# An attention layer in fixed order: its two GRUs as a pipeline, W_gat folded into weights, and 1/degree by logarithm and Newton

## The chip, the cores and the metric

One core of a Trainium2 chip runs the whole program. The metric is device time in microseconds of one execution of the kernel; lower is better. Engines are named as in the profile: PE is TensorE's matrix multiplication and PEld its loading of weights, DVE is VectorE, ACT is ScalarE, POOL is GpSimd and SP is SyncE, which here only issues DMAs. A name with q, such as ACTq, is an engine's own sequencer or DMA queue. L12 is line 12 of the kernel before.

## The reference

Four graph layers in a row work on x (3327 nodes by 64 numbers) with one adjacency matrix of 0 and 1. Each layer is x = x + layer(relu(layernorm(x))). Layers 0 and 3 are hyperbolic attentions; layer 1 is a decaying sum over neighbours; layer 2 is a graph attention with two GRUs. With the weights at hand, the matrix has no negative entries, and this is what layer 2 comes to:

```python
def gru_cell(x, h, w_ih, w_hh, b_ih, b_hh):
    gi = x @ w_ih.T + b_ih
    gh = h @ w_hh.T + b_hh
    ir, iz, inn = jnp.split(gi, 3, axis=1)
    hr, hz, hn = jnp.split(gh, 3, axis=1)
    r = jax.nn.sigmoid(ir + hr)
    z = jax.nn.sigmoid(iz + hz)
    n = jnp.tanh(inn + r * hn)
    return (1.0 - z) * n + z * h
...
node_support = jnp.concatenate([(A_node > 0).astype(h.dtype) @ h, (A_node < 0).astype(h.dtype) @ h], axis=1)
edge_output = gru_cell(node_support, h, w_ih_e, w_hh_e, b_ih_e, b_hh_e)
edge_support = gat(h, A_node, A_edge, W_gat, a_gat)
node_output = gru_cell(edge_support, h, w_ih_n, w_hh_n, b_ih_n, b_hh_n)
return d_edge[:, None] * edge_output + d_node[:, None] * node_output
```

The attention gives all neighbours of a node the same weight here, so that `gat` is (A @ h) @ W_gat divided by the node's degree.

## The kernel before, in words

Nodes are padded to 3328: 26 tiles of 128. The kernel runs four stages, and at the end a count of assumptions (ok) decides whether a slower general version must run as well.

Layer 0 (`hyperbolic_series`, L304) reads the matrix in pieces and lasts until 284 us. Layer 1 (`plain_decay`, L1230) reads it again, in 52 quarters of 832 KB (`quarters`, L1201), keeps it on chip as 13 double tiles of one byte an element (`masks`), and sums with decaying weights. Layer 2 (`plain_gat`, L1374) and layer 3 take it from there.

In `plain_decay` a step is one quarter. DVE makes the mask (L1287), and, for the quarters that are not in the list `LATE` (13 of 52), counts the zeros (`zeros`, L1207), by which the kernel knows that there are only zeros and ones. PE counts neighbours (L1294), ACT takes powers of two (L1300), and PE sums (L1311). The order is written out by hand (`manual_schedule`): each of the named engines does its work in the order of the program, and masks are made two steps ahead. Four quarters are in flight (L1258), one is loaded when a buffer comes free. Ahead of the loop stand the norm (`norm_relu`, L111) and the splitting of its result H into two 16-bit parts (`split2`, L164), and behind it ACT copies the degrees (L1316), a product turns the sums back (L1195) and DVE adds them to X (L1320). POOL adds the bias to X (L1362) and clears the masks' diagonal (L178).

In `plain_gat` the order is not written out: a scheduler arranges the instructions of each engine by priority and readiness. There are these parts:

- the 13 late quarters are read again (L1394), four in flight, for their zero counts;
- the norm and the split of H;
- 416 products of the masks with the two parts of H into four banks (L1407), from the last row tile b = 25 down to 0;
- between them, at two places of that loop, the turning of H into columns (`to_pairs`, L1170), and the degrees: a count of those up to 100 (L1415), their sum (L1416), and for each of four pieces the subtraction of the diagonal (L1424), a clamp to 1 (L1425) and a reciprocal (L1426);
- ACT and DVE take the sums from the banks (L1434, L1435);
- the two GRUs (L1453 to L1475), g = 0 and g = 1, in four pieces of 416 columns each. Two groups of nodes lie in the upper and lower 64 partitions. The second GRU first multiplies its input with W_gat (L1447) and copies it on ACT (L1448);
- the turn back (L1193) and the addition to X (L1482, L1483).

The weights come through POOL's and ACT's DMA queues (`gru_weights`, L1209, and L1251 to L1254). `ball` (L274) makes the constants of a hyperbolic layer; for layer 3 it works from r on DVE (L295 to L301), after the degrees.

Of the kernel before, what the change touches and what calls it, by code (L numbers as in the profile page):

```python
# [46 lines left out]
def tile_gnn4(ctx: ExitStack, tc: tile.TileContext, x, adjT, att0, b0, w1, bias1, w_gat, a_gat,  # L47
# [63 lines left out]
    def norm_relu(pool, h, dst=None):  # L111

        s = pool.tile([P, T], F32, name="ln_s")
        v = pool.tile([P, T], F32, name="ln_v")
        sq = pool.tile([P, T, D], F32, name="ln_sq")
        for ts in HALVES:
            V.reduce_sum(s[:, ts], X[:, ts, :], axis=AX.X)
        V.tensor_scalar(s, s, 1.0 / D, None, op0=OP.mult)
        for ts in HALVES:
            V.tensor_sub(h[:, ts, :], X[:, ts, :], wide(s[:, ts]))  # L120
            A.activation(sq[:, ts, :], h[:, ts, :], AF.Square)
        for ts in HALVES:
            V.reduce_sum(v[:, ts], sq[:, ts, :], axis=AX.X)  # L123
# [3 lines left out]
        for o, ts in enumerate(HALVES):  # L127
            V.scalar_tensor_tensor(h[:, ts, :] if dst is None else dst[:, o], h[:, ts, :], 0.0, wide(sd[:, ts]),
                                   op0=OP.max, op1=OP.mult)

# [33 lines left out]
    def split2(pool, src, name):  # L164

        hi, lo = [pool.tile(list(src.shape), F16, name=f"{name}_{k}") for k in range(2)]
        n = src.shape[1] // 2
        for q in (slice(0, n), slice(n, src.shape[1])):
            A.activation(hi[:, q], src[:, q], AF.Copy, scale=SH)
            V.scalar_tensor_tensor(lo[:, q], src[:, q], SH, hi[:, q], op0=OP.mult, op1=OP.subtract)  # L170
        return hi, lo
# [102 lines left out]
    def ball(att, b_att, r, min_norm, min_norm2, after=None):  # L274

        k = "0" if r is None else "1"
# [13 lines left out]
        if r is None:  # L290
            for t, value in ((cc, 1.0), (sqc, 1.0), (isqc, 1.0), (um, 0.0), (maxn2, min_norm2)):
                V.memset(t, value)
        else:
            nc.scalar.dma_start(cc, bcast_rows(r))
            V.scalar_tensor_tensor(cc, after, -3e38, cc, op0=OP.min, op1=OP.max)  # L295
            V.tensor_mul(cc, cc, cc)
            V.reciprocal(cc, cc)
            V.tensor_copy(sqc, sqrt_(const, cc, "sq"))
            V.reciprocal(isqc, sqc)
            V.tensor_scalar(um, sqc, min_norm / MIN_NORM, None, op0=OP.mult)  # L300
            V.tensor_scalar(maxn2, cc, min_norm2, None, op0=OP.mult)  # L301
        return wlr, bcol, cc, sqc, isqc, um, maxn2

    def hyperbolic_series(r, params, ok, masks=None, done=None):  # L304
# [18 lines left out]
        with ExitStack() as st:  # L323
# [161 lines left out]
            with tc.tile_pool(name="hsw", bufs=2) as wk, tc.tile_pool(name="hsps", bufs=1, space=PSUM) as ps, \  # L485
# [60 lines left out]
                def sums(k):  # L546
# [15 lines left out]
                    if b == T - 1:  # L562
                        a = new("sum", c)
# [606 lines left out]
    def to_pairs(psum, dst, src, lower):  # L1170


        for t0 in range(0, T // 2, 4):
            n = min(4, T // 2 - t0)
            pt = psum.tile([P, 4 * P], F32, name="pt")
            for k in range(n):
                t = t0 + k
                PE.transpose(pt[:, k * P:(k + 1) * P], src[:, t, :, :].rearrange("p o d -> p (o d)"), ident)
            cs = slice(t0 * P, (t0 + n) * P)
            A.activation(dst[:, cs], pt[:, :n * P], AF.Copy)  # L1180
            for o in range(2):
                A.activation(lower[o][D:, cs], pt[o * D:(o + 1) * D, :n * P], AF.Copy)

    def from_pairs(psum, src, use, w=None, tiles=range(T // 2), pt=None):
# [24 lines left out]
    def gru_weights(pool):  # L1209

        wg = pool.tile([P, D], F32, name="wg")
        for o in (0, D):
            nc.gpsimd.dma_start(wg[o:o + D, :], w_gat)
        gru = []
        for wi, wh, bi, bh in ((wih_e, whh_e, bih_e, bhh_e), (wih_n, whh_n, bih_n, bhh_n)):
            g = len(gru)
            wt = pool.tile([P, 3, D], F32, name=f"gw{g}")
            bt = pool.tile([P, 6], F32, name=f"gb{g}")
            brz = pool.tile([P, 3], F32, name=f"gs{g}")
            nc.gpsimd.dma_start(wt[:D, :, :], wi[:D].rearrange("k (g m) -> k g m", g=3))  # L1220
            nc.gpsimd.dma_start(wt[D:, :, :], wh.rearrange("k (g m) -> k g m", g=3))
            for o in (0, D):
                q = slice(o, o + D)
                nc.gpsimd.dma_start(bt[q, :3], bi)
                nc.gpsimd.dma_start(bt[q, 3:], bh)
            G.tensor_tensor(brz, bt[:, :3], bt[:, 3:], op=OP.add)
            gru.append((wt, bt, brz))
        return wg, gru

    def plain_decay(masks, zo, deg):  # L1230
# [8 lines left out]
        K = 200.0  # L1239
        steps = [(c, b) for c in range(2) for b in range(T - 1, -1, -1)]  # L1240
        with ExitStack() as st:
# [7 lines left out]
            wt = pers.tile([P, P], F32, name="wt")  # L1249
            G.memset(wt, 0.0)  # L1250
            nc.scalar.dma_start(wt[:D, :D], w1)  # L1251
            nc.scalar.dma_start(wt[D:, D:], w1)
            bias = pers.tile([P, D], F32, name="bias")
            nc.scalar.dma_start(bias, bcast_rows(bias1, D))  # L1254
            adjs = {}

            def load(k):
                adjs[k] = wk.tile([P, 2, CW], F32, name="adj", bufs=4)  # L1258
                nc.sync.dma_start(adjs[k], quarters(k))

            for k in range(4):
# [9 lines left out]
            with tc.tile_pool(name="pdacc", bufs=1, space=PSUM) as pa, tc.manual_schedule(  # L1271
# [42 lines left out]
                def degrees(c, o):  # L1314
                    q = slice(o * D, (o + 1) * D)
                    A.activation(deg[q, c * CW:(c + 1) * CW].rearrange("p (h i) -> p h i", h=2),  # L1316
                                 cnt[o][q, :, :BK], AF.Copy)
# [11 lines left out]
                make_mask(1)  # L1329
                with tc.tile_pool(name="pdp", bufs=1) as tp:  # L1330
                    H = tp.tile([P, T, D], F32, name="H")
                    norm_relu(tp, H)
                    table_of(AF.Exp)
                    parts = split2(pers, H, "h2")
                for o in range(2):
                    cnt[o] = pa.tile([P, 2, 512], F32, name=f"cnt{o}")
                for k in range(K_ + 2):
# [19 lines left out]
                    if k + 2 < K_:  # L1357
                        make_mask(k + 2)
                        if k + 4 < K_:
                            load(k + 4)  # L1360
                    if k == 4:
                        G.tensor_tensor(X, X, bias[:, None, :].to_broadcast([P, T, D]), op=OP.add)  # L1362
# [11 lines left out]
    def plain_gat(masks, zo, deg, first, wg, gru):  # L1374
# [8 lines left out]
        with ExitStack() as st:  # L1383
            pers = st.enter_context(tc.tile_pool(name="pg", bufs=1))
            H = pers.tile([P, T // 2, 2, D], F32, name="H")
            hP = pers.tile([P, HP], F32, name="hP")

            xh = [pers.tile([P, HP], F32, name=f"xh{o}") for o in range(2)]
            oP = pers.tile([P, HP], F32, name="oP")
            wk = st.enter_context(tc.tile_pool(name="pgl", bufs=4))  # L1390
# [4 lines left out]
            with tc.tile_pool(name="pgp", bufs=1) as tp:  # L1395
                norm_relu(tp, tp.tile([P, T, D], F32, name="hn"), H.rearrange("p k o d -> p o k d"))
                parts = split2(pers, H, "h2")

            with tc.tile_pool(name="pgacc", bufs=1, space=PSUM) as pa, \
                    tc.tile_pool(name="pgps", bufs=2, space=PSUM) as ps:  # L1400
                acc = [pa.tile([P, BK], F32, name=f"acc{k}") for k in range(C)]
                for b in range(T - 1, -1, -1):
# [7 lines left out]
                    if b == T - 3:  # L1410
                        to_pairs(ps, hP, H, xh)
                    if b == T - 4:

                        few = wk.tile([P, HP], BF, name="few", bufs=1)
                        V.tensor_scalar(few, deg, 100.0, 0.0, op0=OP.is_le, op1=OP.add, accum_out=ok[:, 3:])  # L1415
                        V.reduce_sum(zo[:, 2 * T:], deg, axis=AX.X)  # L1416
                        V.tensor_mul(zo[:, 2 * T:], zo[:, 2 * T:], first)
                        for k in range(C):
                            cs = slice(k * BK, (k + 1) * BK)
# [149 lines left out]
```

## Time and profile before

| what | us |
|---|---|
| three runs, median | 829.16 |
| three runs, lowest and highest | 827.92, 830.69 |
| the profiled execution, its own time | 831.17 |
| its span, first to last instruction | 829.5 |
| DVE busy | 721.5 (87% of the span) |
| PE busy | 662.2 (80%) |
| ACT busy | 562.0 (68%) |
| POOL busy | 419.0 (51%) |

The profile is one execution. Busy time of PE is modelled. The shares are averages over stages with different limits, so that a change is to be looked for in its own stage. Layer 0 takes the first 284 us, the decay stage goes on to 429, the attention layer to 543, and layer 3 takes the rest. The chain that ended last, followed back from the last instruction, is 65% DVE, 14% PE, 7% DMA, 6% ACT and 5% issue.

### The profile page before, as it was taken

What the parts mean: (1) busy time and instruction counts of PE and PEld (TensorE: products, weight loads), DVE (VectorE), ACT (ScalarE), POOL (GpSimd) and SP (SyncE); (2) the same over time, 40 slices, a digit from 0 to 9 for tenths busy, and PEclk for the clock granted to TensorE, in tenths of its full rate; (3) what the DMA queues carried; (4) which work ended last, traced back from release to release, by engine and by line L of the source; (5) the groups of instructions that cost most, each with busy time, mean ns of one, the idle gap of its engine ahead of it and who ended that gap; (6) DMA issues with size and microseconds to landing.
All of it is one profiled execution on the core that took longest, in us unless ns stands there. A gap on an engine that the chain in (4) does not pass through costs nothing.

```text
span 829.5 us, 11810 instructions
## 1 busy us (share of the span) xinstructions
PE 662.2 (80%) x4228; PEld 251.2 (30%) x4228; DVE 721.5 (87%) x1013; ACT 562.0 (68%) x684; POOL 419.0 (51%) x283
## 2 busy tenths in 40 slices
PE   0889999999896059989970997618999999998940
PEld 0422233333331024435430662204222333333310
DVE  7689999999997999999989946796999999999966
ACT  3878888888884167777761306448888888888850
POOL 2499989989985310002300000004787777787720
PEclk9999999999999569999995899958999999999985
DMA  2577766767662639999943630002001001000001
GB/s 42 167 235 227 204 204 191 238 182 204 190 191 66 225 126 339 349 347 333 338 170 126 220 113 1 0 0 48 1 2 35 1 1 35 0 2 1 0 4 44
DMA packets 56887, 107.86 MB, mean 130 GB/s; under 512 B 8305, under 2 KB 32817, under 8 KB 56817
## 3 DMA queue, kind: packets, MB, share of 16 engines
q1 hardware_dynamic: 51712, 106.68, 40.2%
q10 hardware_dynamic: 4656, 0.08, 0.3%
q8 instruction: 35, 0.57, 0.3%
q0 software_dynamic: 448, 0.24, 0.1%
q14 instruction: 36, 0.29, 0.1%
HBM read 103.73 MB, written 0.88 MB: 126 GB/s over the span
## 4 chain that ended last, share of the span: by engine, by line
DVE 65%; PE 14%; DMA 7%; ACT 6%; issue 5%; POOL 2%; ACTq 1%; DVEq 0%; POOLq 0%
DVE sig L543 22%; DVE slot L542 20%; DMA adj<-in 7%; DVE same L1207 5%; PE acc L1407 5%; DVE mask L1287 3%; POOL sig L519 2%; PE slot L552 2%; ACT y L537 1%; DVE deg L1426 1%; PE cnt L1294 1%; DVE X L740 1%; DVE prod L739 1%; PE slot L560 1%; DVE ln_v L123 1%
## 5 line engine op out<-in xcount | busy, mean ns | idle before, releaser
L537 ACT ACTIVATE y<-slot,shift_c 128x768 f32<-128x768 f32 (+1 forms) x208 | 197.6, 950 | 69.7 <-ACT sig L517 48.1
L543 DVE TENSOR_TENSOR sig<-slot,sig 128x768 f32<-128x768 f32 (+1 forms) x208 | 213.2, 1025 | 24.7 <-POOL sig L519 2.7
L542 DVE SCALAR_TENSOR_TENSOR slot<-y,slot 128x768 f32<-128x768 f32 (+1 forms) x208 | 212.1, 1020 | 9.0 <-ACT y L537 8.9
L519 POOL TENSOR_TENSOR sig<-adj,sig 128x768 f32<-128x768 f32 (+1 forms) x104 | 201.8, 1962 | 24.8 <-ACT sig L517 14.7
L517 ACT ACTIVATE sig<-leftB,right 128x768 f32<-128x768 f32 (+1 forms) x208 | 204.1, 981 | 0.2
L519 POOL TENSOR_TENSOR sig<-mask,sig 128x768 f32<-128x768 fp8e4 (+1 forms) x104 | 174.6, 1680 | 57.2 <-ACT sig L517 53.1
L552 PE MATMUL slot<-sig,Xr 128*64 128x384 f32 (+1 forms) x832 | 187.2, 538 | 18.3 <-DVE sig L543 18.3
L530 PE MATMUL slot<-XC,XT 128*128 128x384 f16 (+1 forms) x416 | 142.1, 342 | 5.0 <-DVE sig L543 3.3
L531 PE MATMUL slot<-XF,XE 73*128 73x384 f16 (+1 forms) x416 | 141.4, 340 | 0.0
L1300 ACT ACTIVATE w<-cnt,ebias 128x832 bf16<-128x832 f32 x104 | 93.8, 950 | 32.4 <-PE cnt L1294 32.4
L1207 DVE TENSOR_SCALAR_CACHE_REDUCE same<-adj 128x1664 bf16<-128x1664 f32 x52 | 97.7, 1880 | 3.5 <-DMA adj<-in 3.5
L560 PE MATMUL slot<-sig,X 128*32 128x384 f32 (+1 forms) x832 | 95.0, 529 | 0.0
L468 POOL COPY Xp<-Xe 128x234 f16<-128x234 f16 x2 | 0.8, 415 | 160.1 <-DVE XT L414 146.4
L552 PEld LDWEIGHTS slot<-sig,Xr 128*64 128x64 f32 x832 | 42.9, 135 | 123.9 <-DVE sig L543 85.2
L1294 PE MATMUL cnt<-mask,after 128*128 128x416 fp8e4 x208 | 54.8, 347 | 25.3 <-DVE mask L1287 22.6
L178 POOL TENSOR_TENSOR mask<-mask,offdiag 128x128 fp8e4<-128x128 fp8e4 x26 | 16.8, 666 | 105.4 <-PE cnt L1294 104.2
L530 PEld LDWEIGHTS <-XT 128*128 128x128 f16 x416 | 40.6, 98 | 94.7 <-issue 68.8
L1294 PE MATMUL cnt<-mask,rest 128*128 128x416 fp8e4 x208 | 55.0, 347 | 12.5 <-ACT w L1300 12.5
L1287 DVE TENSOR_SCALAR mask<-adj 128x1664 fp8e4<-128x1664 f32 x52 | 53.3, 1031 | 6.7 <-DMA adj<-in 6.6
L531 PEld LDWEIGHTS <-XE 73*128 73x128 f16 x416 | 40.7, 98 | 33.3 <-issue 9.3
L1311 PE MATMUL acc<-w,h 128*64 128x416 bf16 x416 | 47.2, 349 | 0.0
L1407 PE MATMUL acc<-mask,h 128*64 128x416 fp8e4 x416 | 38.3, 346 | 0.1
(293 smaller groups left out, 547.7 us busy)
## 6 DMA issues: line engine op xcount, KB each, us to landing
adj<-in SPq DMA_DIRECT2D x65, 832.0 KB, 6.9
adj<-in SPq DMA_DIRECT2D x78, 384.0 KB, 3.9
adj<-in SPq DMA_DIRECT2D x27, 512.0 KB, 4.7
leftB<-left SPq DMA_DIRECT2D x6, 384.0 KB, 3.9
XC<-XT SPq DMA_DIRECT2D x12, 96.0 KB, 3.0
X<-in SPq DMA_DIRECT2D x1, 832.0 KB, 4.5
out<-X SPq DMA_DIRECT2D x2, 416.0 KB, 2.4
XF<-XT SPq DMA_DIRECT2D x6, 96.0 KB, 2.7
```

Of the source, the lines that this page charges most:

```text
L517: A.activation(sig, leftB[c], AF.Sigmoid, bias=right[:, b:b + 1])
L519: G.tensor_tensor(sig, adj, sig, op=OP.mult)
L530: PE.matmul(L[:, o, :c[1] * P], XT[:, rows], XC[c][:, o, :], start=True, stop=False)
L531: PE.matmul(L[:, o, :c[1] * P], XE[:KE, rows], XF[c][:, o, :], start=False, stop=True)
L537: A.activation(ys[k], Ls[k][:, :, :c[1] * P], AF.Square, scale=-0.5 / SX ** 2, bias=shift_c)
L542: V.scalar_tensor_tensor(L, y, G3, L, op0=OP.add, op1=OP.mult)
L543: V.tensor_mul(sig, L, sig)
L552: PE.matmul(acc[c][o * D:(o + 1) * D, 0, :n], Xr[:, b, :], sigs[k][:, o, :], start=b == 0, stop=b == T - 1)
L560: PE.matmul(acc[c][q:q + 32, 1, :n], X0[:, b - 1 + i, :], w[:, o, :], start=b == 1, stop=b == T - 1, tile_position=(0, q))
L1207: V.tensor_scalar(same, adj, 0.0, 0.0, op0=OP.is_equal, op1=OP.add, accum_out=count)
L1294: PE.matmul(cnt[o][:, h, :BK], w, cols(k, o, h), start=w is after and steps[k][1] == T - 1, stop=True, skip_group_check=True)
L1300: A.activation(ws[k][:, o, :, :], cnt[o][:, :, :BK], AF.Exp, scale=-LN2, bias=ebias)
```

## The change

All of layer 2 after the loads is put into one region of fixed order for ACT, DVE and PE.

- `norm_relu` takes an order of its halves and a function that runs after each, so that the second half of H, which the products need first, is split first; in layer 1 too, where the other half's split is put into step 1 of the loop.
- W_gat is multiplied into the second GRU's input weights once (a transpose, a product and two copies), and the product L1447 is gone.
- The degrees' work is spread over the product loop by a table of places (`todo`). The reciprocal becomes a logarithm and an exponential on ACT and one step of Newton in two DVE operations; the count of large degrees goes to ACT, and their sum to the copies in layer 1.
- The eight GRU steps run as a pipeline over eight banks.
- In layer 1, seven quarters are in flight instead of four, and the bias is added in 13 pieces. In layer 2, three late quarters instead of four.
- All weights are loaded through SP's queue at the start (16 DMAs), and the constants of layer 3 come from r by powers on POOL, in layer 1.

The core of the diff:

```diff
-    def norm_relu(pool, h, dst=None):
+    def norm_relu(pool, h, dst=None, order=(0, 1), then=None):
...
+        for o in order:
+            ts = HALVES[o]
             V.scalar_tensor_tensor(h[:, ts, :] if dst is None else dst[:, o], h[:, ts, :], 0.0, wide(sd[:, ts]),
                                    op0=OP.max, op1=OP.mult)
+            if then is not None:
+                then(o)
...
+            def of_r():
+                G.tensor_tensor(cc, cc, cc, op=OP.mult)
+                for i, (to, src) in enumerate(((cc, cc), (sqc, cc), (isqc, cc))):
+                    G.tensor_tensor(to, src, half[:, i:i + 1], op=OP.pow)
...
+    def middle_weights():
...
+            nc.sync.dma_start(wx[:D, :, :], wi[:D].rearrange("k (g m) -> k g m", g=3))
+            nc.sync.dma_start(wx[D:, :, :], wh.rearrange("k (g m) -> k g m", g=3))
...
+        AHEAD = 7
...
-                                 cnt[o][q, :, :BK], AF.Copy)
+                                 cnt[o][q, :, :BK], AF.Copy, accum_out=zo[q, 2 * T + c:2 * T + c + 1])
...
+                def after_norm(o):
+
+                    if o == 1:
+                        table_of(AF.Exp)
+                        ts = HALVES[1]
+                        split2(*[p[:, ts, :] for p in parts], H[:, ts, :])
...
+                    if k == 1:
+                        late()
+                    if 3 <= k < 3 + T // 2:
+
+                        ts = slice(2 * (k - 3), 2 * (k - 2))
+                        G.tensor_tensor(X[:, ts, :], X[:, ts, :], bias[:, None, :].to_broadcast([P, 2, D]), op=OP.add)
...
-            wk = st.enter_context(tc.tile_pool(name="pgl", bufs=4))
+            wk = st.enter_context(tc.tile_pool(name="pgl", bufs=3))
...
+                norm_relu(tp, hn, H.rearrange("p k o d -> p o k d"), order=(1, 0),
+                          then=lambda o: split2(*[p[:, :, o, :] for p in parts], H[:, :, o, :]))
+
+                pt = bank(4)
+                PE.transpose(pt[:D, :D], wg, ident[:D, :D])
+                A.activation(wgT, pt[:D, :D], AF.Copy)
+                pt = bank(5)
+                wx = gru[1][0]
+                PE.matmul(pt[:D, :3 * D], wgT, wx[:D, :, :].rearrange("k g m -> k (g m)"), start=True, stop=True)
+                A.activation(wx[:D, :, :].rearrange("k g m -> k (g m)"), pt[:D, :3 * D], AF.Copy)
...
+                def inverse():
+
+                    few = hn.rearrange("p t d -> p (t d)")
+                    r0 = tp.tile([P, T, D], F32, name="ln_sq").rearrange("p t d -> p (t d)")
+                    V.tensor_scalar(zo[:, 2 * T:], zo[:, 2 * T:], first, None, op0=OP.mult)
+                    V.tensor_scalar(deg, deg, 1.0, None, op0=OP.max)
+                    A.activation(few, deg, AF.Relu, bias=hundred, accum_out=ok[:, 3:])
+                    A.activation(r0, deg, AF.Ln)
+                    A.activation(r0, r0, AF.Exp, scale=-1.0)
+                    table_of(AF.Sigmoid, r0[:, :1])
+                    V.scalar_tensor_tensor(deg, deg, -1.0, r0, op0=OP.mult, op1=OP.mult)
+                    V.scalar_tensor_tensor(deg, deg, 2.0, r0, op0=OP.add, op1=OP.mult)
+
+                todo = {T - 4: lambda: turn(0), T - 6: lambda: degrees(0), T - 8: lambda: turn(4),
+                        T - 9: lambda: degrees(1), T - 11: lambda: turn(8), T - 12: lambda: degrees(2),
+                        T - 14: lambda: turn(12), T - 15: lambda: degrees(3), T - 17: inverse}
...
-                    if b == T - 3:
-                        to_pairs(ps, hP, H, xh)
...
-                            V.reciprocal(deg[:, cs], deg[:, cs])
+                    if b in todo:
+                        todo[b]()
                     if b % 2 == 0:
                         same = wk.tile([P, 2, CW], BF, name="same", bufs=1)
                         k = LATE[(T - 1 - b) // 2]
                         zeros(same, late.pop(0), zo[:, k:k + 1])
...
+                    pg[u] = pr, pz, ph, pi = [bank((4 + 4 * u + i) % 8)[:, :BK] for i in range(4)]
...
+                def before_tanh(u):
+                    bt = gru[steps[u][0]][1]
+                    nn = nns[u] = tp.tile([P, BK], F32, name="nn", bufs=3)
+                    V.scalar_tensor_tensor(nn, pg[u][2], bt[:, 5:6], gates[u][0], op0=OP.add, op1=OP.mult)
+                    V.tensor_add(nn, nn, pg[u][3])
...
+                def state(u):
+                    g, k = steps[u]
+                    cs = slice(k * BK, (k + 1) * BK)
+                    nn = nns[u]
+                    o = tp.tile([P, BK], F32, name="o", bufs=1)
+                    V.tensor_sub(o, hP[:, cs], nn)
+                    if g == 1:
+                        V.tensor_add(nn, nn, oP[:, cs])
+                    V.tensor_mul(o, o, gates[u][1])
+                    V.tensor_add(oP[:, cs], o, nn)
+
+                take(0)
+                for u in range(K + 2):
+                    if u < K:
+                        products(u)
+                    if u == 0:
+                        take(1)
+                    if u < K:
+                        sigmoids(u)
+                    if u == 0:
+                        take(2)
+                        take(3)
+                    if 0 <= u - 1 < K:
+                        tanh(u - 1)
+                    if u < K:
+                        before_tanh(u)
+                    if u < C:
+                        take2(u)
+                    if 0 <= u - 1 < K:
+                        state(u - 1)
```

`turn(t0)` transposes four tiles of H and copies them on ACT five times (once to hP, and to the lower half of the inputs of each of two GRUs and two groups); `degrees(k)` is the diagonal's product and its subtraction; `take(k)` copies the sums of bank k on ACT and scales them with 1/degree on DVE; `take2(k)` copies that to the second GRU's inputs on ACT; `products(u)`, `sigmoids(u)` and `tanh(u)` are the PE and ACT parts of step u.

## The prediction

> **What bounds the kernel now.** I first read the busy time by stage, to find the stages that the diff touches. Columns: stretch, its length, then busy time and instructions of PE, PEld, DVE, ACT and POOL, the granted clock, the DMA share, GB/s.
>
> ```profile
> 298.00:429.00 131.00, 125.68 (x840) 57.02 (x839) 121.41 (x132) 98.30 (x111) 16.81 (x26) 0.97 0.86 300
> 429.00:458.00 29.00, 5.38 (x31) 3.69 (x33) 28.08 (x35) 6.67 (x11) 0.00 (x0) 0.65 0.41 147
> 458.00:498.00 40.00, 39.49 (x422) 24.51 (x418) 26.44 (x43) 6.95 (x15) 0.00 (x0) 0.95 0.48 172
> 498.00:539.00 41.00, 29.63 (x152) 9.49 (x152) 27.57 (x49) 22.31 (x40) 0.00 (x0) 0.96 0.00 0
> ```
>
> The decay stage (298 to 429) is PE-bound, with DVE close behind. The next 29 us belong to DVE alone. Then PE is full for 40 us, and in the GRUs (498 to 539) no engine is. The chain of waits names the work in the second stretch:
>
> ```profile
> 434.67 1.89 DVE same L1207 x2
> 436.56 1.86 DVE ln_s L117 x2
> ...
> 443.57 2.66 DVE deg L1426
> ...
> 447.26 2.61 DVE deg L1426
> ...
> 450.87 2.65 DVE deg L1426
> ...
> 453.93 1.87 DVE H L128 x2
> 456.03 1.69 ACT h L169 x2
> 457.76 1.60 PE acc L1407 x8
> ...
> 465.02 32.49 PE acc L1407 x368
> ```
>
> The norm, which PE waits for, shares DVE with three of the four reciprocals, and stands behind a zero count. PE's 416 products start at 457.76 only. In the GRUs I read DVE's timeline (start, length, idle before in brackets); the first of these lines is the first GRU's first step, the others are the second GRU's:
>
> ```profile
> 506.19 0.65 DVE L1465 SCALAR_TENSOR_TENSOR nn<-ph,gb,spr 128x416 f32<-128x416 f32 x1 [4.34 <-PE ph L1463]
> ...
> 524.32 0.65 DVE L1465 SCALAR_TENSOR_TENSOR nn<-ph,gb,spr 128x416 f32<-128x416 f32 x1 [0.68 <-PE ph L1463]
> ...
> 529.39 0.65 DVE L1465 SCALAR_TENSOR_TENSOR nn<-ph,gb,spr 128x416 f32<-128x416 f32 x1 [0.68 <-PE ph L1463]
> ```
>
> The second GRU takes 5.07 us a step, with DVE waiting for PE, which waited for ACT's copy of the W_gat product. In the first GRU the same row starts at 506.19, 509.31, 512.17 and 515.11: 2.95 us a step, DVE full.
>
> **What the Trainium skill says.** (1) "ScalarE: Activation LUTs", What ACT_TABLE_LOAD costs: a load is 1283 ns, an ACTIVATE 186 ns plus 0.833 ns an element, 93 more for a pointer bias. The trace agrees: loads of 1.28 us, and 1.57 us for the 1664-wide L433. (2) The same page, Table sets: one set holds both exp and ln. No run here shows it. (3) "SBUF — State Buffer", SBUF: two separate sides: GpSimd and some VectorE forms share a port pair, locked for a whole instruction. The trace agrees: a 26-element operation that usually takes 0.18 us took 1.79 while POOL added the bias (3.69 us, from 290.45):
>
> ```profile
> L124 DVE TENSOR_SCALAR ln_v<-ln_v x4: 114/180/1790, 12.2 to 549.1; 128x26 f32<-128x26 f32 x4
> ```
>
> (4) "TensorE: Matmul & The Clock Gate", Part 1: a PE that has been idle runs at half clock for some 3.4 us of work. Here 36 products took 4.14 us (115 ns each) from 460.6, and 368 took 32.49 (88 ns each) afterwards.
>
> **The change part by part**, on the clock of the trace of before.
>
> *Start of the program.* Sixteen weight DMAs go to SP's queue behind X's load, before layer 0's first transfers. SP has nothing to issue until 26.4, and at some 0.5 us an issue (13 KB of left: 0.57 us) they end near 10, so the queue hides them. But ACT's own DMA issues hold the chain at the start (4.16 us for one at L280; ACT is free for the norm's first square at 9.31, DVE gave it at 8.6), and transfers that share the engines may delay them. Layer 3's four small DMAs already sit in that queue (6.87 to 9.26). From 0.7 gained by another order to 4 lost; I take +0.5. The weight loads on POOL's queue, now at 266 to 284, go away; DVE works alone there until 284.3, so this gives nothing.
>
> *Decay stage.* PE needs 2.34 us a step (its sums start at 305.78, 308.12, 310.45 and so on), DVE 0.94 + 1.80, or 0.94 for the late quarters, on average 2.29. Seven quarters in flight remove DVE's 6.6 us of waiting for DMA, but PE hides nearly all of that: only the last three steps go at DVE's 2.79, 2.74 and 2.74, which is 1.25 us over PE's pace. Those are gained. The pause at 360 to 365 is PE waiting for ACT's copies of the degrees and stays; an accumulator on them costs 0.1 each (DVE's read takes 0.08), two on the path: +0.2. At the stage's start one half of the split (0.91 on ACT) instead of two stands ahead of the first weights: 0.9 gained. The other half, 0.91 on ACT and 0.93 on DVE in step 1, lies in steps that PE, still at half clock, makes slow. The bias in 13 pieces does not wait for the loop: POOL is in order and X is free at 290.45, so the pieces run there too, and each of DVE's eight small operations can meet one (3.69/13 = 0.28 plus overhead). I put the port's stall where it was, 1.6 us; bounds 0 and 3. The powers on POOL have no reader before 555 and POOL is idle until 367: nothing, whatever they cost. Sum -2.0, from -5 to +0.5.
>
> *From the decay's end to the first GRU operation.* Without the two degree counts (1.89 + 1.88) and the zero count (1.89) ahead of it, the norm starts when X is complete: PE's last transpose ends at 432.1, plus an add of 0.6: 432.75. By the decay prologue's rows, less the stall: sums 1.87, scale 0.2, two differences, squares and their sums to 6.25 after the start, root and reciprocal to 7.85, first half of H 8.85, ACT's high part 9.8, DVE's low part 10.8, second half of H 11.75, ACT 12.7. ACT is in order, so the copy of W_gat's transpose comes only then (0.3), and PE's product with it (0.4) stands ahead of the 416. They start at 432.75 + 13.45 = **446.2**, 11.6 earlier than before. They take 416 x 88 ns = 36.7, 13 transposes some 2.0, the degree products 0.7, half clock for 5 us 2.5: **488.1**.
>
> DVE is worse off. It does two zero counts (1.93 each), then waits at each degree subtraction for PE to come to its place in the order; the fourth comes 26.5 after 446.2, at 472.7. Then 0.6, a zero count 1.9, the clamp and a scalar 1.2: 476.4. It now waits for ACT: count 1.75, table load 1.28, logarithm 1.57, exponential 1.57: 482.6. Newton is two operations of the 1664-wide form, 1.87 each: 486.4. Behind that stand five zero counts. Three go at once; the fourth needs a load issued when a buffer came free at 488.3, 5 us away (the first late load took 5.78), and the fifth lands at 495.5. **DVE is free at 497.5**, 9 us after PE. Behind it four scalings (0.52 each), so the first GRU operation is at 499.6, against 506.19: **-6.6**. Two table sets instead of one: +1.3. Loads of 6.9 us, the page's median: +1.9. The zero counts off the path: -5.6 (a rival below). Before, the same counts (460 to 487) lay under PE.
>
> *GRUs.* 506.19 to 538.73 was 32.5. Now, an in-order alternation: DVE makes one step's first two operations while ACT makes the sigmoids of the next, and finishes the step before. Operations that depend on their predecessor start 0.60 to 0.68 apart, others 0.51. A first-GRU step is 0.68 + 0.52 + 0.63 + 0.62 + 0.52 = 2.97 (2.95 was seen), a second-GRU step 0.52 more, with overlap 3.38: 4 x (2.97 + 3.38) = 25.4. PE needs 2.4 a step (505.96 to 508.4) and has two sets of four banks; ACT at most 1.1 + 0.55 + 1.0 = 2.65. So DVE hides both: **-7.1**, W_gat's products (4 x 0.7) and eight copies being off the path, and the sigmoid table, loaded at 501.93 before, under DVE's wait. What follows (542.96 on) is unchanged.
>
> **Sum** against the profiled execution, 831.17 (span 829.5 and 1.67 around it): +0.5 - 2.0 - 6.6 - 7.1 = -15.2, giving 816.0. That execution was 2.0 above the median of the three runs, so I predict **814.0**.
>
> **Rivals.** (a) DVE's tail does not delay the GRUs: the zero counts slip into its waits, and PE's end sets the start, at 488.1 + 5.9 (two takes, products, sigmoid, two more takes, as in 497.0 to 506.2 less the table load and the waits) = 494.0; the port's stall goes too. -7.2: 806.8. For it: DVE has 26.4 of 40 us busy now. Against it: a fixed order cannot fill a wait. (b) The second GRU keeps 5.07 us a step, because ACT, in order between two steps, holds each tanh behind the next sigmoids: 4 x 1.69 = +6.8: 820.8. For it: ACT's spare is only 0.3 a step. (c) Slower: the fixed order makes every step a round trip, sigmoid 0.6, two operations 1.28, tanh 0.65, state 1.85, products 2.4: 6.8 a step, 54.4 for eight instead of 25.4: 843. That needs bank reuse to chain each product to the state before it; the point where it loses all the gain is (25.4 + 15.2)/8 = 5.07 us a step. Against it: the first GRU ran at 2.95 with two buffers a tile. (d) The deeper prefetch does nothing, as PE holds the loop: only +1.2, inside the range.
>
> **How the numbers follow.** Forecast 0.58, (a) 0.15, (b) 0.18, (c) 0.09. The range runs from below (a) to above (b), with the start's +4 added to the forecast and the decay's -5 taken off: 804 to 824; (c) and some tails are out. About 0.3% (2.5 us) is what a measurement can tell from no change: a quarter of (b), with a bad start, falls there. Faster 0.87, same 0.04, slower 0.09.
>
> **What would show it.** PE's products should start about 11.5 us after the decay's last add, and end some 9 us before DVE's last zero count. Five zero counts should stand after the Newton pair. First-GRU steps should go at about 3.0, second at 3.4. The decay's last steps should go at 2.34. It is wrong if PE's products are interrupted, if a GRU step nears 5 us, or if layer 0 begins several us late.

## The result, and the profile after

| | before | after |
|---|---|---|
| median of five runs, us | 829.16 | 822.11 |
| lowest and highest, us | 827.54, 830.69 | 820.08, 822.82 |
| span of the profiled execution, us | 829.5 | 820.4 |

The ratio is 0.9908, with a 95% interval of [0.9894, 0.9922]. The medians differ by 7.05 us, where 15.2 were forecast. The forecast's direction and range held; about half of its gain came. Line numbers from here on are those of the changed kernel; in the experiments they are shifted by a few.

Busy time by stage of the changed kernel (columns as in the prediction):

```profile
429.00:458.00 29.00, 13.59 (x119) 8.27 (x117) 16.32 (x24) 10.11 (x18) 0.00 (x0) 0.76 0.42 148
458.00:498.00 40.00, 34.08 (x359) 20.34 (x355) 25.70 (x28) 22.02 (x34) 0.00 (x0) 0.96 0.51 171
498.00:539.00 41.00, 22.17 (x125) 7.80 (x126) 36.85 (x68) 18.32 (x32) 0.00 (x0) 0.71 0.00 1
```

PE now works in the second stretch (13.59 us instead of 5.38), but from 458 to 498 DVE is busy for 25.70 of 40 us only, though the GRUs wait for DVE at the end of it. The chain of waits of the changed kernel says for what (start, length, what):

```profile
446.63 0.12 ACT wgT L1420
...
473.64 0.04 DVE deg L1447
...
478.98 1.28 ACT L1456
...
481.88 1.28 ACT L1457
...
492.38 6.60 DMA adj<-in
...
501.63 3.04 PE bank L1505 x8
504.68 1.25 PE bank L1510 x8
```

PE's products begin behind ACT's copy of W_gat's transpose (L1420). The fourth degree subtraction (L1447) stands behind PE. L1456 and L1457 are two table loads, one for the logarithm and one for the exponential. Then a late load of adj is waited for, and at last PE's products of the second GRU step, at half clock (the granted clock is 0.50 from 501.63 to 504.60, and 1.00 from 505.80). DVE's timeline shows that last wait, and that from there the pipeline runs as forecast:

```profile
502.90 0.64 DVE L1523 SCALAR_TENSOR_TENSOR nn<-bank,gb,gate 128x416 f32<-128x416 f32 x1
...
506.03 0.65 DVE L1523 SCALAR_TENSOR_TENSOR nn<-bank,gb,gate 128x416 f32<-128x416 f32 x1 [1.87 <-PE bank L1510]
...
508.97 0.65 DVE L1523 SCALAR_TENSOR_TENSOR nn<-bank,gb,gate 128x416 f32<-128x416 f32 x1
```

The difference of the spans, cut at four marks that both traces have:

| from, to | before | after | change | forecast |
|---|---|---|---|---|
| start, first mask of the decay | 284.34 | 286.14 | +1.80 | +0.5 |
| first mask, last sums of the decay | 143.55 | 142.28 | -1.27 | -2.0 |
| last sums, first GRU operation | 78.30 | 74.48 | -3.82 | -6.6 |
| first GRU operation, end of the last | 32.54 | 27.74 | -4.80 | -7.1 |
| the rest | 290.77 | 289.76 | -1.01 | 0 |

The sum is -9.1 where -15.2 was forecast. The remaining 2.0 us between -9.1 and the medians' -7.05 are those by which the profiled execution of before lay above its median.

### The profile page after: what moved, and what is told of

Read it like the earlier page. It is cut to its first block, busy times and chain, and to the rows that moved or that the text cites. A ratio compares the mean times of both kernels' runs of the same rounds, so it can differ in the third digit from the quotient of the medians.

```text
span 820.4 us, 11781 instructions
## 1 busy us (share of the span) xinstructions
PE 659.6 (80%) x4215; PEld 250.7 (31%) x4215; DVE 709.0 (86%) x999; ACT 574.5 (70%) x704; POOL 413.5 (50%) x286
## 5 line engine op out<-in xcount | busy, mean ns | idle before, releaser
L525 POOL TENSOR_TENSOR sig<-adj,sig 128x768 f32<-128x768 f32 (+1 forms) x104 | 201.9, 1962 | 24.4 <-ACT sig L523 15.2
L179 POOL TENSOR_TENSOR mask<-mask,offdiag 128x128 fp8e4<-128x128 fp8e4 x26 | 15.0, 593 | 99.6 <-PE cnt L1285 97.7
L429 PE MATMUL junk<-Xp,ident_h 128*128 128x512 f16 x20 | 6.7, 478 | 41.1 <-ACT Xp L406 41.1
```

The lines of the kernel that those rows point to most:

```text
L525: G.tensor_tensor(sig, adj, sig, op=OP.mult)
```

## Experiments

Each kernel is the change with one edit, unless said otherwise, and was timed in five rounds against the kernel before; ratios are to that, and the change itself has 0.9908. 0.0012 of a ratio is 1 us.

**Theory.** The GRUs start late because DVE's fixed order chains it to PE (four subtractions), then to ACT (logarithm), and only then lets it do five zero counts and the takes. **Rivals**: PE's own end, the late loads, or the price of the reciprocal sets the start.

### Zero counts while ACT works (e1_newton_last)

```diff
-                    V.scalar_tensor_tensor(deg, deg, -1.0, r0, op0=OP.mult, op1=OP.mult)
-                    V.scalar_tensor_tensor(deg, deg, 2.0, r0, op0=OP.add, op1=OP.mult)
+                    def newton():
+                        V.scalar_tensor_tensor(deg, deg, -1.0, r0, op0=OP.mult, op1=OP.mult)
+                        V.scalar_tensor_tensor(deg, deg, 2.0, r0, op0=OP.add, op1=OP.mult)
+                    last.append(newton)
...
                         zeros(same, late.pop(0), zo[:, k:k + 1])
+                last[0]()
```

> The five zero counts that stand behind the Newton pair on DVE are put ahead of it; nothing else is moved. Theory (DVE's fixed order delays the GRUs): they fill DVE's 7.7 us of waiting for ACT, the pair ends near 493 instead of the last count at 500.9, and the first GRU operation comes at about 495.5 instead of 502.9: 7 to 8 us faster than the changed kernel, some 814.5. Rival (the GRUs wait for PE's sums or for ACT, and the zero counts only happen to be there): within 1 us of the changed kernel, some 822.

Measured: 813.99, ratio 0.9806 [0.9788, 0.9823]. DVE's timeline, first in the change, then here:

```profile
484.80 1.89 DVE L1459 SCALAR_TENSOR_TENSOR deg<-deg,ln_sq 128x1664 f32<-128x1664 f32 x1 [7.70 <-ACT ln_sq L1457]
```

```profile
487.71 1.89 DVE L1200 TENSOR_SCALAR_CACHE_REDUCE same<-adj 128x1664 bf16<-128x1664 f32 x1 [1.64 <-DMA adj<-in]
...
491.59 1.89 DVE L1463 SCALAR_TENSOR_TENSOR deg<-deg,ln_sq 128x1664 f32<-128x1664 f32 x1
```

The five counts stand where DVE waited for ACT, Newton follows without a wait, and the first GRU operation is at 497.51, 62.8 after the norm's start (69.3 in the change). The theory holds: the order alone cost some 8 us by the medians, and 6.5 in the profiled execution, which lay 1.5 above its median. The late loads have a part in what is left: the five counts wait 3.8 us for them.

### The degrees ahead of the norm (e2_early_degrees)

```diff
+                dgs = [bank(k)[:, :BK] for k in range(C)]
+                for k in range(C):
+                    for o in range(2):
+                        PE.matmul(dgs[k][o * D:(o + 1) * D, :], ones_bf[:, :D],
...
+                    A.activation(hi, src, AF.Copy, scale=SH)
+                    for k in ((0, 1) if o == 1 else (2, 3)):
+                        V.tensor_sub(deg[:, cs], deg[:, cs], dgs[k])
...
+                todo = {T - 4: lambda: turn(0), T - 8: lambda: turn(4), T - 9: lambda: last[0](),
+                        T - 11: lambda: turn(8), T - 14: lambda: turn(12)}
+                inverse()
```

The eight products stand before the norm, the subtractions beside the splitting of H, and the logarithm before the loop. 

> The degrees' products go ahead of the norm, where PE is idle, their subtractions into DVE's two waits for ACT in the split, clamp, logarithm and exponential directly behind the split, the Newton pair behind the fourth zero count. Theory: DVE loses its 11.2 us of waiting for PE and 7.7 for ACT, its last zero count ends before PE's products do, and PE's end sets the GRUs: first GRU operation near 494, the second without its 1.9 us wait: 10 us faster than the changed kernel, some 812. Rival (PE's loop is the bound already): only the 0.7 us of degree products that leave the loop, some 821.5.

Measured: 809.2, ratio 0.9757 [0.9741, 0.9774]. DVE's timeline in this kernel:

```profile
483.55 0.21 DVE L1604 TENSOR_REDUCE ok<-zo 128x1 f32<-128x54 f32 x1
487.13 0.59 DVE L1501 SCALAR_TENSOR_TENSOR deg<-bank,deg 128x416 f32<-128x416 f32 x1 [3.37 <-ACT xh L1500]
```

Now DVE is done at 483.6 and waits for the sums: PE's end (486.5) sets the start, as rival (a) of the prediction said of the change. The first GRU operation comes 59.9 us after the norm's start, 9.4 earlier than in the change, and the second step no longer waits. In the profiled execution the decay was 1.6 shorter as well, which this edit doesn't touch; of that below (e11_no_sum).

### A plain reciprocal in the same place (e3_reciprocal)

```diff
-                    A.activation(r0, deg, AF.Ln)
-                    A.activation(r0, r0, AF.Exp, scale=-1.0)
-                    table_of(AF.Sigmoid, r0[:, :1])
+                    table_of(AF.Sigmoid)
+                    V.reciprocal(deg, deg)
```

The two lines of Newton go too. 

> The logarithm, the exponential and the Newton pair are taken out and one DVE reciprocal of 1664 columns put in their place; the order stays. Theory: in this place DVE waits for ACT or works, which comes to the same: four times 2.69 is 10.8 us in place of 7.7 of waiting and 3.8 of Newton, so within 1 us of the changed kernel, some 821.5. Rival (the replaced reciprocal is what the change gains): slower than the changed kernel by the 7 us that DVE works longer, some 829.

Measured: 822.57, ratio 0.9907 [0.9891, 0.9923]: no difference. The reciprocal takes DVE 10.55 us, and the logarithm's way (two loads of 1.28, two activations of 1.59, Newton's 3.7, all on the chain) takes 9.5; in the trace the first GRU operation comes 70.2 after the norm's start, 0.9 later than in the change. With DVE only waiting for ACT, moving work to ACT gained nothing that the medians show. In the order of e1 it should pay, as the counts fill that wait; no run has the reciprocal there.

### W_gat's products ahead of the norm (e5_wgat_first)

The block from `pt = bank(4)` to the second copy stands before `norm_relu`. 

> The two products with W_gat and their two copies on ScalarE stand ahead of the norm. Theory (TensorE's start sets the tail through the degree subtractions): in the kernel after the change ScalarE's copies of them end at 448.04, and the first product starts at 447.6, 3.9 us after the first half is split at 443.7. With them out of the way the products, the first degree subtraction (458.66) and the first GRU operation (502.90) come 3 to 4 us earlier: about 818.5. Rival (the late loads of adj or ScalarE's logarithm set the tail, not TensorE's start): the waits on the DMA, 1.49 and 1.42, grow by what the rest gains, and the time stays within 1 us of 822.

Measured: 818.59, ratio 0.9886 [0.9867, 0.9905]. In the trace PE's products start 10.0 after the norm's start instead of 14.0, and the first GRU operation comes 65.4 after it, 3.9 earlier: the theory's place and size. The ratio shows 1.8 of it, and its interval overlaps that of the change, so the median alone would not settle it.

### The takes ahead of the last two zero counts (e10_takes_earlier)

```diff
-                        zeros(same, late.pop(0), zo[:, k:k + 1])
+                        if b > 2:
+                            zeros(wk.tile([P, 2, CW], BF, name="same", bufs=1), late.pop(0), zo[:, k:k + 1])
+                        else:
+                            held.append(k)
```

The held counts follow `take(3)`. 

> The change, but DVE's last two zero counts stand behind the four takes of the sums, ahead of the first GRU operation. Theory (TensorE's products of the second step need the banks that the takes release, and stand idle because the takes stand behind two late loads): the takes come at 494.2 in place of 500.90, the second step's wait of 1.87 goes, one wait for a load (1.49) is filled, the other (landing at 499.1) stays: first GRU operation at 501, 3 to 4 us in all, a ratio of 0.986 to before, about 818.3. Rival (the second step's wait is ScalarE's or TensorE's own length, not the banks): the wait stays, at most 1.5 us gained, 0.989 or more.

Measured: 817.42, ratio 0.9861 [0.9836, 0.9886]. DVE's timeline:

```profile
493.93 2.08 DVE L1494 SCALAR_TENSOR_TENSOR deg<-bank,deg 128x416 f32<-128x416 f32 x4
...
500.53 0.65 DVE L1526 SCALAR_TENSOR_TENSOR nn<-bank,gb,gate 128x416 f32<-128x416 f32 x1
...
501.72 0.64 DVE L1526 SCALAR_TENSOR_TENSOR nn<-bank,gb,gate 128x416 f32<-128x416 f32 x1
```

PE's timeline at the second step's products, in the change and then here:

```profile
501.63 3.04 PE L1505 MATMUL bank<-xh,gw 128*64 128x416 f32 x8 [9.48 <-DVE deg L1491]
```

```profile
494.66 3.04 PE L1508 MATMUL bank<-xh,gw 128*64 128x416 f32 x8 [2.77 <-DVE deg L1494]
```

The second step follows the first by 1.2 us in place of 3.1. In both kernels its products start when the takes release the banks, as the theory says. But their own length has a part too: they take 4.2 us in the change and 4.0 here, at half clock after PE's pause, where those of later steps take 2.5. The difference is about the wait of 1.87. Here two zero counts stand between the takes and the first GRU operation, and the slow products lie under them. In e1_newton_last, where nothing stands there, they take 4.1 and the second step still waits 1.77. So the wait came of the late takes and of the half clock behind PE's pause together; this edit hides it and does not tell the two apart.

### Layer 3's small loads on SP's queue (e4_ball_on_sp)

```diff
+        q = nc.scalar if r is None else nc.sync
-                nc.scalar.dma_start(wc[o * D:(o + 1) * D, :],
+                q.dma_start(wc[o * D:(o + 1) * D, :],
```

The two other loads likewise. 

> Layer 3's four small DMAs go from ACT's queue to SP's; the sixteen weight DMAs stay on SP. Theory (the start is 1.8 us later because ACT issues all its DMAs before its table load, its memset and the norm's first square): the first square at 9.3 instead of 11.5, 2 us faster than the changed kernel, some 820. Rival (the sixteen weight DMAs on SP's queue hold up the transfers): no gain, or worse with twenty of them, 822 or more.

Measured: 819.79, ratio 0.988 [0.9859, 0.9902]. ACT's timeline, first in the change, then here:

```profile
8.94 0.44 ACTq L296 DMA_DIRECT2D cc<-in  x1
9.41 1.28 ACT L371 ACT_TABLE_LOAD   x1 [9.41 <-issue]
```

```profile
6.33 0.61 ACTq L291 DMA_DIRECT2D bcol<-in  x1
6.96 1.28 ACT L372 ACT_TABLE_LOAD   x1 [6.96 <-issue]
```

In the change ACT issues all its DMAs ahead of its first computation, which starts 2.4 us later than here. Twenty DMAs on SP's queue do not hold up the start, so that the rival is out. In the nine kernels of this study with this queue the decay's first mask lies at 285.4 to 287.3 (mean 286.3), in the four with the loads on SP's at 283.7 to 284.7 (mean 284.2). The ratio's interval overlaps that of the change; it is these traces that show the 2 us.

### No overlap of GRU steps (e6_serial_gru)

```diff
-                for u in range(K + 2):
...
+                for u in range(K):
+                    products(u)
...
+                    before_tanh(u)
+                    tanh(u)
...
+                    state(u)
```

> The same GRU operations, but each step's tanh and state directly after its gates, before the next step's products are issued: no overlap of two steps. Theory (the pipeline is what took the step from 3.67 and 5.07 down to 2.94 and 3.44, since DVE works without a gap): DVE waits once a step for the tanh and once for the gates; steps of 4.3 to 5, with 9 steps some 10 to 13 us more than after: 832 to 835, all of it between the first and the last GRU operation. Rival (DVE's own work sets the step in any order, as only the wait for gates counts): under 3 us more, 825.

Measured: 824.69, ratio 0.9949 [0.9933, 0.9966]: 3.4 us more than the change. The rival has the number, and my theory the wrong price. DVE's timeline:

```profile
506.46 0.59 DVE L1524 TENSOR_TENSOR nn<-nn,bank 128x416 f32<-128x416 f32 x1
507.76 0.59 DVE L1534 TENSOR_TENSOR o<-hP,nn 128x416 f32<-128x416 f32 x1 [0.71 <-ACT nn L1527]
```

A step waits 0.71 for the tanh and for nothing else, because PE and ACT prepare the next step's gates in another set of banks in any case: 3.73 and 4.24 us a step. First to last GRU operation is 31.96, against 32.54 before and 27.74 in the change, so overlap is what took the 4.2 us away. (The change's 27.74 has the second step's wait in it, which is hidden here; against the 25.9 of e2_early_degrees, which doesn't wait there, overlap is worth 6.1.) The second GRU is 17.0 here and 19.5 before, which I put down to W_gat in the weights. The first is 14.9 here and 13.1 before, since the kernel before already overlapped it: its first steps took 2.9 to 3.1, and the 3.67 of my text stands in no trace.

### Four quarters in flight again (e7_ahead4)

`AHEAD = 4` in place of 7. 

> The decay loads adj 4 ahead in place of 7, as before the change. Theory (TensorE sets the loop, the deeper prefetch only moves the start): the loads of the first tiles still come in time, and the loop's span is within 1 us of after; 821 to 823.5. Rival (the prefetch is what gained in the decay's first steps): the sums start 2 to 3 us later and the whole comes to 825 or more.

Measured: 824.57, ratio 0.9942 [0.9925, 0.9959]: 2.8 more than the change. Neither text is right: the sums start where they did (305.24 and 305.18), but from there the decay takes 125.7 instead of 123.2. DVE waits eight times for a load, 3.9 in all, as here, where the change does not wait at all:

```profile
418.00 1.05 DVE L1278 TENSOR_SCALAR mask<-adj 128x1664 fp8e4<-128x1664 f32 x1 [0.84 <-DMA adj<-in]
```

Not all of these 2.5 are the prefetch's. Four steps are 0.2 to 0.35 longer, 1.1 in all, which fits masks that come late. Another 1.1 lies at the pause for the degrees, where more of PE's work runs at half clock: three steps of 5.88, 4.41 and 2.69 instead of 5.54, 3.97 and 2.34. e3_reciprocal has the same there (5.88, 4.41, 2.75) with seven quarters in flight. So what I can put down to the prefetch itself is 1.1, and rival (d) of the prediction, that it does nothing, is out by that much. Nor are the decay's last steps all its doing: with four in flight they go at 2.34, 2.34 and 2.55 here, and at 2.79, 2.74 and 2.74 in the kernel before.

### Without the sum over the degrees' copies (e11_no_sum)

```diff
-                                 cnt[o][q, :, :BK], AF.Copy, accum_out=zo[q, 2 * T + c:2 * T + c + 1])
+                                 cnt[o][q, :, :BK], AF.Copy)
```

Two columns that the sum would have filled are cleared instead. 

> The change without the sum over ScalarE's copies of the degrees in layer 1 (it leaves out that sum, which only the check of the degrees reads). Theory (each sum is followed by a read of 0.19, TensorE's wait at the pause grows from 1.64 to 1.84, and it goes on at half clock): the step after the pause is 2.33 again in place of 3.97, the pause 5.24 in place of 5.53, and the decay ends 0.2 to 0.4 sooner after its last sums: 2.0 to 2.3 us less, a ratio of 0.988 to before, about 820. Rival (the half clock comes of the pause itself, whatever its last 0.2): the step stays near 3.9, 0.4 to 0.7 gained, 0.990.

Measured: 5367.36. Without that sum the program's own count of assumptions calls for the slower general version as well, so the time says nothing; layer 1 in the trace does. PE's timeline, in the change and then here:

```profile
364.83 0.51 PE L1285 MATMUL cnt<-mask,after 128*128 128x416 fp8e4 x2 [1.84 <-ACT deg L1307]
365.27 1.58 PE L1302 MATMUL acc<-w,h 128*64 128x416 bf16 x8
...
369.24 0.89 PE L1302 MATMUL acc<-w,h 128*64 128x416 bf16 x8
```

```profile
364.74 0.51 PE L1285 MATMUL cnt<-mask,after 128*128 128x416 fp8e4 x2 [1.64 <-ACT deg L1307]
365.18 0.89 PE L1302 MATMUL acc<-w,h 128*64 128x416 bf16 x8
367.52 0.89 PE L1302 MATMUL acc<-w,h 128*64 128x416 bf16 x8
```

With the accumulator's read (0.19 on ACT) PE waits 0.2 longer, and then works at half clock: eight products in 1.58 instead of 0.89, at a granted clock of 0.51. The step takes 3.97 instead of 2.34, and the decay is 1.9 longer. Of the twelve kernels here with the sum, eleven have such a step (3.5 to 4.4). That the sum brings it on is likely, but not shown: e2_early_degrees has 2.34 after the same wait of 1.85. And e2_early_degrees and this kernel are the only two of all fourteen that ran the decay's very first eight sums at full clock (0.89; 1.2 to 1.6 in the others), so that they may share a state of the clock in which the sum has no part. For the sum speaks the kernel before: it has 1.59 there, waits 1.64 at the pause, and goes on at 2.34. All this fits the Trainium skill, "TensorE: Matmul & The Clock Gate", Part 1: The HAM clock gate, by which the clock is set by activity in a free-running window; the same gap could then fall either way. That the window is the cause was not tested.

### The three edits together (e8_all)

> Degrees summed ahead of the norm, the ball's small loads on SyncE's queue, and W_gat's products first, in one kernel. If the three costs are separate (start 1.4 to 2.3, subtractions chained to TensorE 13, W_gat's products 3.5): 809.2 - 2.3 - 3.5 = 803.5. If the tail is by then set by the loads of adj alone, W_gat's part is lost: about 807.

Measured: 805.94, ratio 0.9727 [0.9714, 0.9741]. The start's part came: the decay's first mask is at 283.68, 2.5 earlier than in e2_early_degrees. W_gat's part hardly came: PE began 10.0 after the norm's start, 4.0 earlier, but then stood and waited for DVE, and the first GRU operation is 58.8 after the norm's start (59.9 in e2_early_degrees). PE's timeline:

```profile
442.63 0.90 PE L1481 MATMUL bank<-mask,h 128*64 128x416 fp8e4 x4 [8.03 <-ACT h L1433]
445.12 7.49 PE L1481 MATMUL bank<-mask,h 128*64 128x416 fp8e4 x60 [1.59 <-DVE deg L1436]
```

The products need banks 0 to 3, in which the degree sums still waited to be subtracted.

### The degree sums in banks of their own (e9_own_banks)

```diff
-                dgs = [bank(k)[:, :BK] for k in range(C)]
+                dgs = [bank(4 + k)[:, :BK] for k in range(C)]
```

The edit is against e8_all. 

> The three edits together as before (degrees early, the ball's loads on SyncE's queue, W_gat's products first), but the degree sums in banks 4 to 7, where the products do not accumulate. Theory (in the version with banks 0 to 3 TensorE stood 1.59 us for DVE's second pair of subtractions, and some 0.9 more between, and TensorE's end at 486.1 sets the GRUs): the products run from 442.6 without a break and all that follows comes 2 to 2.5 us earlier, a ratio of 0.970 and about 803.6. Rival (the late loads, whose last zero count ends at 483.4, take over): under 1 us, 0.972.

Measured: **803.64**, ratio 0.9686 [0.9661, 0.9711]: the fastest level of the study, 3.1% under before. PE's timeline:

```profile
441.51 7.57 PE L1481 MATMUL bank<-mask,h 128*64 128x416 fp8e4 x64 [7.73 <-ACT h L1433]
```

The products run without a break, and the first GRU operation comes 56.4 after the norm's start, 2.4 earlier than in e8_all. That is the theory's size; the late loads do not take over.

### The bias after the first masks (e12_bias_later)

```diff
+                    if k == 3:
+                        bias2 = pers.tile([P, D], F32, name="bias2")
+                        V.tensor_copy(bias2, bias)
```

The 13 pieces add bias2; the base is e9_own_banks. 

> The version of all three edits with own banks, in which GpSimd's 13 bias pieces now wait for a copy of the bias that DVE makes in step 3 of the decay. Theory (the pieces beside the norm and the first masks lengthen DVE's operations on a shared port): H is 1.02 twice in place of 1.25 and 1.27, the first two masks 1.02 in place of 1.27 and 1.12, and the two steps of 2.73 and 2.75 become 2.34: 0.8 us less, 0.9676 and 802.8. Rival (the pieces then meet later masks and cost the same there): no change, 0.9686.

Measured: 803.34, ratio 0.9684 [0.9668, 0.9701], the same as its base. DVE's timeline, in the base and then here:

```profile
298.33 1.27 DVE L1279 TENSOR_SCALAR mask<-adj 128x1664 fp8e4<-128x1664 f32 x1
```

```profile
297.87 1.02 DVE L1279 TENSOR_SCALAR mask<-adj 128x1664 fp8e4<-128x1664 f32 x1
```

The stretched operations are gone, and the eighth sums come 0.8 sooner after the norm, as the theory says; later only one mask is touched (1.13). 0.8 us is 0.1%, too little for the medians to show. This agrees with point (3) of what the prediction took from the skill: DVE's operations were held up beside POOL's, here by 0.1 to 0.25 each.

## Why the prediction was right in direction and half off in size

**Start: +1.80, not +0.5.** Its range named the case ("transfers that share the engines", up to 4) but not the cause. I let SP's 16 DMAs hide, and they did, though the last is issued at 16.7 and not near 10; I took ACT's order as it was before, where the table load stood ahead of layer 3's loads. In the change it stands behind all of them (e4_ball_on_sp).

**Decay: -1.27, not -2.0.** The sum came near, but partly by luck: two errors had opposite signs. The last steps go at 2.34, as forecast; that gained 1.25, though the prefetch, by which I explained it, comes to 1.1 in all, most of it elsewhere in the loop (e7_ahead4). "An accumulator costs 0.1 each, two on the path: +0.2" was too small: its read takes 0.19, and the pause with the step behind it takes 9.51 instead of 7.58, +1.9, of which 1.6 is the step at half clock. Whether the accumulator brings on the half clock is not settled (e11_no_sum). Against this, the way from the first mask to the first sums was 2.3 shorter, where I had 0.9. The port's stall, which I had left where it was, changed its form: DVE's small operations were free (L126 takes 0.18 where L124 once took 1.79), but H and the first masks were stretched by 0.1 to 0.3 each, 0.8 in all (e12_bias_later).

**From the last sums to the first GRU operation: -3.82, not -6.6.** The mechanism was the forecast's: PE ended at 489.1 and DVE was last, at 500.9. Several terms were 2.8 too small together. The prologue to PE's products took 14.0 rather than 13.45, and the copies ahead of it 0.3 more (the products themselves gave 0.5 back). "Two table sets instead of one: +1.3" was kept as a bound, and is what happened: the Trainium skill, "ScalarE: Activation LUTs", Table sets, has one set with exp and ln, but this program loads a table before the exponential too (1.28 at 481.88). And the late loads made DVE wait 1.49 and 1.42 where I had allowed 1.5 for both. Whether four of them in flight, as before, would have come in time, no run shows. One sign in "What would show it" was mistaken already in its own text: 11.5 us from the last add to PE's products should have read 13.45; 14.0 was measured. And in point (4) from the skill the 36 products from 460.6 show the half clock badly: the granted clock there is 0.88. The eight from 457.76 show it: 1.60 us, at a granted clock of 0.50.

**GRUs: -4.80, not -7.1.** Steps of 2.94 and 3.44 were forecast as 2.97 and 3.38, and rivals (b) and (c) are out. What I left out is the pipeline's filling: the second step's products need banks that four takes on DVE release, and DVE came to them last; PE stood for 9.48 and then worked at half clock (e10_takes_earlier). That cost 1.87. Without this wait the eight steps take 25.9 (e9_own_banks), 0.5 above my 25.4. In the kernel before, too, DVE was not quite full in the first GRU: it waited 0.27 to 0.71 for each tanh.

**Rivals.** (a) was wrong for the change, and right once the chain to PE was cut: e9_own_banks runs at what (a) describes, and, with its start mended too, is faster than (a) said, 803.6 to 806.8. The change as it stands left 18 us lying in the order of its instructions, the queue of four DMAs and a choice of banks.

What stays open: what sets PE's clock after the pause, and the 1.0 us of the last row. In layer 3 only the place of its constants and the number of buffers of one tile were changed. From its norm on it takes 286.5 before and 285.3 in the change, but 283.6 to 285.3 in the twelve kernels whose layer 3 is the same, so that a part of this is spread between executions.

## What to carry to other kernels

In a fixed order, ask of each waiting instruction what stands behind it on its engine: here ten us of independent counts stood behind a wait for ACT, and moving two lines (e1_newton_last) gained more than the whole change had. Put the operations that depend on another engine's place in a loop ahead of that loop, and give their results banks that the loop doesn't use. A DMA that a computing engine issues can hold up that engine's start (2.4 us here), and an instruction that is moved may come to stand behind it.

## What the runs showed of the hardware that was not expected

- Reading ACT's accumulator takes 0.19 us as an instruction of its own, and PE's wait is 1.84 with it instead of 1.64. In eleven of the twelve kernels with such a read a step of 3.5 to 4.4 instead of 2.34 follows; why is open (e11_no_sum).
- After a pause of 2.7 to 10.6 us ahead of the second GRU step PE's sixteen products took 4.0 to 4.6 us, and 2.5 in later steps (nine kernels).
- Powers on POOL over 128x1 take 0.55 to 0.57 us each, and up to 1.70 in e12_bias_later, where DVE's masks and zero counts run beside them.
- Thirteen bias pieces take POOL 8.6 us (0.46 and 8.12), where one operation had taken 3.69.
